# A four-layer transformer stack on one core: reciprocals spread by ScalarE, a shorter guess, a shorter matrix series

## The chip, the cores and the metric

One Trainium2 core. A core has five engines that run side by side, each with its own queue in order: TensorE (PE in the profile, with its weight loads as PEld), VectorE (DVE), ScalarE (ACT), GpSimd (POOL) and SyncE (SP, which issues DMAs). They meet only at semaphores. The metric is the device time of one execution in microseconds, lower is better.

## The reference

`x` is (32, 128, 144): 32 sequences of 128 tokens with 144 channels, all fp32. Four layers are applied one after the other, each conditioned on one vector per sequence:

```python
# layer 0: adaLN block; q and k are normalised per head (16 heads of 9)
qkv = (ln(x) * (1 + sc) + sh) @ w_qkv + b_qkv
q, k = ln(q) * g_q, ln(k) * g_k                 # over the 9 channels of a head
attn = softmax(q @ k.T * 9**-0.5)
x = x + g_msa * ((attn @ v) @ w_proj + b_proj)
x = x + g_mlp * (gelu(mod(ln(x)) @ w1 + b1) @ w2 + b2)

# layer 1: a rotation per sequence in a subspace of 64 directions
U, _ = qr(P)                                    # P is 144 x 64
R = expm(A)                                     # A: 64 x 64, skew, from the condition
x = x + (x @ U @ R - x @ U) @ U.T

# layers 2 and 3: adaLN blocks like layer 0 without the norm of q and k;
# layer 3 has a mixture of 4 experts, 2 per token, in place of the MLP
```

## The kernel before

The program is written in one recorded order, which every engine follows for its own instructions; no scheduler reorders it. The order comes from a table of *ticks*. In each tick three sequences are at three stages of attention: `s0` gets its first scores (for the row maxima), `s1` its second scores (maxima subtracted) and exponentials, `s2` its weighted sums and the projection out. One sequence enters each tick. Layer 0, here called the first block, takes 32 ticks and the few around them; layers 2 and 3 follow. A tick has named gaps ("a", "e", "b", "den", "c", "y1", "d", "z" and so on), and the table puts other work into them: layer norms, projections to q, k, v for later sequences, the MLP of earlier ones.

In a tick of the first block, after the second half of the scores (L841, with two reductions on VectorE, L846, and two exponentials on ScalarE, L853), gap "c" issues `qk0_T` for the next sequence (four transpositions, L771, and three scalings on ScalarE, L774 to L776) and `qk0_project` for a later one (L686 and L687 on TensorE, then two operations on ScalarE, L729 and L730). `divide_T` follows gap "c", `divide` follows gap "y1", `largest_T` and `largest` stand near the end, and `project_out` (L932) closes the tick.

The softmax division works in transposed form. `sums` transposes the weighted sums (L881), takes the reciprocals of the 16 denominators per token on VectorE (`rd`, L884) and spreads each one over the 16 columns of its slot (`rdx`, L886). `divide_T` transposes the spread tile back on TensorE (L906), into the bank of the sums, and `divide` multiplies (`oT`, L911). `project_out` uses `oT`.

The norm of q and k in layer 0 needs a reciprocal root per head. `qk0_variance` sums the squares, `qk0_guess` makes the integer guess (a shift right by one, then a subtraction from a constant, both on VectorE) and `qk0_newton` improves it three times on GpSimd.

Layer 1's matrices are prepared during the first block, in pieces. `prep_qr` makes the QR by 64 Householder columns, three pieces per column, six pieces per tick. `prep_expm` makes the matrix exponential: a scaling by a power of two (`THETA`, `NSQ`, `NSQ1`), the powers of the squared matrix, two series of eight terms (`even`, `odd`) in two halves of four (`hi`, `lo`), and four squarings (L561). It gets one piece in gap "b" and one in gap "z" of a tick; each `yield` ends a piece. A branch (L586) would add fourteen squarings if a matrix had a norm over `THETA * 2**4`. When both are done, `prep_rot` (L601) joins them; what is left by tick 30 is done there at once.

Of the kernel before, what the change touches and what calls it, by code (L numbers as in the profile page):

```python
# [8 lines left out]
F32 = mybir.dt.float32  # L9
U32 = mybir.dt.uint32  # L10
I32 = mybir.dt.int32
AF = mybir.ActivationFunctionType
ALU = mybir.AluOpType
# [20 lines left out]
EPS = 1e-6  # L34
SCALE = HD**-0.5

THETA = 2.0
NSQ = 18
NSQ1 = 4
KP = 80  # L40
# [10 lines left out]
SLOT = 16  # L51
ONE = HD
RSQRT = 0x5F3759DF
# [13 lines left out]
def tile_kernel(ctx: ExitStack, tc: tile.TileContext, a: dict, out: bass.AP):  # L67
    nc = tc.nc
# [4 lines left out]
    work = ctx.enter_context(tc.tile_pool(name="work", bufs=2))  # L73
# [45 lines left out]
    def mat(name, tag=None):  # L119

        tag = tag or name

        if tag in ("pow1", "pow2"):
            at0 = MLP_COLS + 1024 * (tag == "pow2")
            return mlps[:, at0 : at0 + 1024].rearrange("p (b d) -> p b d", d=D)
        if tag in ("pow3", "pow4"):
            return pw34[:, int(tag == "pow4")]
        if tag in ("hi", "even_lo"):
            at0 = 4 + 2 * (tag == "hi")
            t = hid[:, at0 : at0 + 2].rearrange("p a i t -> p (a i t)")  # L130
            return t.rearrange("p (b d) -> p b d", d=D)
        return pe.tile([128, NB2, D], F32, tag=tag, name=name)
# [261 lines left out]
    def prep_expm():  # L394
# [9 lines left out]
        i2b = cst[:, K_I2 : K_I2 + D].unsqueeze(1).to_broadcast([128, NB2, D])  # L404
# [102 lines left out]
        def products(lhs, rhs, name, take):  # L507

            for c in range(2):
                ps = bank([128, 512], f"{name}_{c}")  # L510
                product(ps, lhs, rhs, c)
                take(
                    slice(c * NB4, (c + 1) * NB4), ps.rearrange("p (b d) -> p b d", d=D)
                )
                yield

        fact = [1.0]
# [3 lines left out]
        pw1, pw2, pw3, pw4 = (mat(f"pow{n}") for n in range(1, 5))  # L521
# [5 lines left out]
        def series(co, name):  # L527

            lo, hi = mat(f"{name}_lo"), mat(f"{name}_hi", "hi")
            for t, cs_ in ((hi, co[4:]), (lo, co[:4])):  # L530
                nc.vector.tensor_scalar(t, pw1, cs_[1], None, ALU.mult)
                yield
                for c, x in ((cs_[0], i2b), (cs_[2], pw2), (cs_[3], pw3)):
                    nc.vector.scalar_tensor_tensor(t, x, c, t, ALU.mult, ALU.add)
                    yield
            yield from products(
                pw4, hi, f"ps_{name}",
                lambda bs, ps: nc.vector.tensor_tensor(lo[:, bs, :], lo[:, bs, :], ps, ALU.add),
            )
            return lo  # L540

        even = yield from series([(-1.0) ** k / fact[2 * k] for k in range(8)], "even")
        odd = yield from series([(-1.0) ** k / fact[2 * k + 1] for k in range(8)], "odd")
        rot, rotT = mat("rot", "pow3"), mat("rotT", "pow4")

        def sum_and_difference(bs, ps):
# [62 lines left out]
    st = defaultdict(dict)  # L609
# [129 lines left out]
    def qk0_guess(s):  # L739
        va = st[s]["va"]  # L740
        y = small.tile([128, 32], F32, tag="qky", name=f"qky_{s}", bufs=2)
        nc.vector.tensor_scalar(
            y.bitcast(I32), va.bitcast(I32), 1, None, ALU.logical_shift_right
        )
        nc.vector.tensor_scalar(y.bitcast(I32), y.bitcast(I32), -1, RSQRT, ALU.mult, ALU.add)
        st[s]["y"] = y

    def qk0_newton(s, eng=nc.gpsimd):
# [128 lines left out]
    def sums(s):  # L877

        po = st[s]["ot"][:, : 2 * T].rearrange("p (t q) -> p t q", t=2)
        for t in range(2):  # L880
            nc.tensor.transpose(po[:, t, :], st[s]["on"][:, t, :], ident)  # L881
        den = po.rearrange("p t (s c) -> p t s c", c=SLOT)[:, :, :, ONE]
        rd = small.tile([128, 2, 8], F32, tag="rd", name=f"rd_{s}")
        nc.vector.reciprocal(rd, den)  # L884
        rdx = work.tile([128, 2, 8, SLOT], F32, tag="rdx", name=f"rdx_{s}")
        nc.vector.tensor_copy(rdx, rd.unsqueeze(3).to_broadcast([128, 2, 8, SLOT]))  # L886
        st[s]["rdx"] = rdx

    def sums_by_blocks(s):

# [10 lines left out]

    def divide_T(s):
        po = st[s]["ot"][:, : 2 * T].rearrange("p (t q) -> p t q", t=2)
        rdx = st[s].pop("rdx")
        for t in range(2):
            nc.tensor.transpose(po[:, t, :], rdx[:, t, :, :].rearrange("p s c -> p (s c)"), ident)  # L906

# [215 lines left out]
    def load_L3():  # L1123

        t, at0 = rotU.rearrange("p b c -> p (b c)"), 0
        for k in ("wqk", "wqkR", "wv", "wvR", "wproj", "b2"):
# [11 lines left out]
            setattr(L3, k, v)  # L1138

    prep_qr, prep_expm = prep_qr(), prep_expm()  # L1140
    g2 = const.tile([128, 1], F32, name="g2")

# [40 lines left out]
    def prepare_expm(tick, gap):  # L1183
        nonlocal prep_expm
        if prep_expm and (tick >= 0 and gap in ("b", "z") or (tick, gap) == (-2, "z")):
            said = next(prep_expm, 0)
            if said == 0:
                prep_expm = None
            elif said is not None:
                rot_T.append(said)  # L1190
# [26 lines left out]
    for layer in range(3):  # L1217
        ahead = 5 if layer == 0 else 6
        for n in range(NG):
            g = (layer, n)  # L1220
            t0 = first[layer] + n * G
            for i in range(G):
                s = layer * B + n * G + i
# [17 lines left out]
                if layer == 0:  # L1241
                    put(t0 + i - 3, "c", qk0_project, s)
                    put(t0 + i - 3, "z", qk0_variance, s)
                    put(t0 + i - 2, "e", qk0_guess, s)
                    if s == 0:
                        for gap in "bbc":
                            put(-2, gap, qk0_newton, s, nc.vector)
                    else:
                        for gap in ("b", "c", "y2"):
                            put(t0 + i - 2, gap, qk0_newton, s)  # L1250
                    put(t0 + i - 1, "b", qk0_divide, s)
                    put(t0 + i - 1, "c", qk0_T, s)
# [62 lines left out]
    for tick in range(-6, first[2] + B + 14):  # L1315
# [20 lines left out]
        if s2 is not None and not joined:  # L1336
            sums(s2)
# [5 lines left out]
        if s2 is not None and not joined:  # L1343
            divide_T(s2)
# [30 lines left out]
def constants():  # L1375
# [9 lines left out]
    for h in range(2):  # L1385
        c[:, K_THR + h * NSQ + t] = np.where(t < NSQ1, -1.0, THETA * 2.0**t)
        c[:, K_WTS + h * NSQ + t] = -(2.0 ** -(t + 1.0))
# [136 lines left out]
```

## Time and profile before

| | |
|---|---|
| runs | 1351.33, 1355.53, 1358.17 us (median 1355.53) |
| profiled execution | 1347.1 us, span of the instructions 1345.4 us |
| TensorE | 1275.4 us busy (95%), weight loads 935.1 (70%) |
| VectorE | 821.9 us (61%) |
| ScalarE | 821.3 us (61%) |
| GpSimd | 642.6 us (48%) |
| granted TensorE clock, mean | 0.993 |

The three runs lie within 7 us of each other, and the profiled execution a little below them. Engines' busy times are over the whole span; the first block, with the preparation of layer 1 beside it, reaches to about 440 us of it. Matmuls are pipelined and the ends of their rows are modelled, so a busy TensorE is not one at its peak. In a line of the trace, `L906` is a line of the kernel, the tile written stands ahead of the arrow, and brackets tell how long the engine sat idle before it and what ended that.

### The profile page before, as it was taken

Reading aid. Unit: us, or ns where it says so; the run is one execution under the profiler, and the core shown is the slowest. Engines: PE = TensorE matmul, PEld = TensorE weight load, DVE = VectorE, ACT = ScalarE, POOL = GpSimd, SP = SyncE. Lnnn points to the kernel's source line nnn. Section 1 sums busy time; section 2 is a strip of 40 time slices with the busy share of each in tenths; the row PEclk is TensorE's granted clock in tenths of the full one; section 3 lists DMA queues with packets and bytes.
Section 4 is the critical chain, followed back from the end, with each engine's and each line's share of the span. In section 5 each row is a group of like instructions: output and inputs, shape, how many; then the busy total and the mean of one; then the engine's idle time right before and its main releaser. Section 6 shows DMA issues by size and latency. Waiting matters only on the chain.

```text
span 1345.4 us, 35550 instructions
## 1 busy us (share of the span) xinstructions
PE 1275.4 (95%) x14172; PEld 935.1 (70%) x14172; DVE 821.9 (61%) x2546; ACT 821.3 (61%) x1804; POOL 642.6 (48%) x1651
## 2 busy tenths in 40 slices
PE   5999898999999989999999999999999999999997
PEld 4678587787776566766777767667676767677765
DVE  5788888867754466666766676645454545454322
ACT  2667777778856565667766666655555555555431
POOL 5677777666644333433434343526261616151632
PEclk9999999999999999999999999999999999999999
DMA  8200000000020000000100000201000000000000
GB/s 235 51 2 19 20 19 2 20 20 4 19 100 31 19 11 19 19 10 19 53 15 15 19 19 9 76 1 28 1 24 5 19 10 19 10 19 2 19 9 9
DMA packets 21671, 34.40 MB, mean 26 GB/s; under 512 B 2304, under 2 KB 12448, under 8 KB 21248
## 3 DMA queue, kind: packets, MB, share of 16 engines
q1 hardware_dynamic: 20848, 31.68, 7.9%
q8 instruction: 114, 1.87, 0.6%
q10 hardware_dynamic: 656, 0.42, 0.1%
q14 instruction: 53, 0.43, 0.1%
HBM read 29.62 MB, written 2.47 MB: 24 GB/s over the span
## 4 chain that ended last, share of the span: by engine, by line
PE 66%; DVE 7%; ACT 1%; issue 1%; POOL 0%; POOLq 0%; DVEq 0%
PE ps_h L665 19%; PE ps_f L1085 8%; PE ps_s L841 6%; PE ps_qk L665 6%; PE ps_o L868 5%; PE ps_w L841 5%; PE ps_f L958 4%; DVE nm L846 3%; PE ps_pj L932 3%; PE ps_v L665 2%; PE ps_f L1089 1%; PE ps_o L800 1%; DVE block L897 1%; DVE oT L899 1%; DVE kT L719 1%
## 5 line engine op out<-in xcount | busy, mean ns | idle before, releaser
L846 DVE TENSOR_REDUCE nm<-ps_s 128x4 f32<-128x512 f32 x384 | 246.3, 682 | 88.4 <-PE ps_w L841 77.2
L853 ACT ACTIVATE pr<-ps_w 128x512 f32<-128x512 f32 x384 | 208.6, 595 | 134.4 <-PE ps_w L841 132.9
L841 PE MATMUL ps_w<-q,kT 32*128 32x128 f32 x3072 | 234.3, 284 | 0.9 <-DVE kT L719 0.9
L841 PE MATMUL ps_s<-kT,qT 32*128 32x256 f32 x1536 | 231.5, 406 | 0.7 <-ACT kT L776 0.6
L841 PEld LDWEIGHTS ps_w<-q,kT 32*128 32x128 f32 x3072 | 197.6, 187 | 12.8 <-issue 6.2
L952 ACT ACTIVATE hid<-ps_h 128x512 f32<-128x512 f32 (+1 forms) x224 | 119.1, 591 | 105.4 <-PE ps_h L665 105.2
L918 POOL TENSOR_TENSOR x_sb<-x_sb,res_a 128x144 f32<-128x144 f32 x96 | 47.1, 490 | 255.9 <-DVE res_a L921 255.1
L841 PEld LDWEIGHTS ps_s<-kT,qT 32*128 32x128 f32 x1536 | 135.1, 184 | 28.6 <-issue 8.2
L665 PE MATMUL ps_h<-hM_m,mlps 128*128 128x512 f32 x304 | 143.8, 606 | 0.0
L1093 DVE SCALAR_TENSOR_TENSOR acc<-ps_f,cw,acc 128x144 f32<-128x144 f32 x128 | 46.6, 366 | 158.6 <-PE ps_f L1089 72.2
L868 PE MATMUL ps_o<-pr,vaug 128*32 128x128 f32 x3072 | 104.8, 277 | 0.6 <-issue 0.6
L868 PEld LDWEIGHTS ps_o<-pr,vaug 128*32 128x32 f32 x3072 | 78.6, 110 | 34.9 <-PE ps_w L841 18.5
L665 PEld LDWEIGHTS ps_h<-hM_m,mlps 128*128 128x128 f32 x304 | 53.5, 190 | 65.6 <-issue 64.2
L958 PE MATMUL ps_f<-mlps,hid 128*128 128x144 f32 x640 | 93.3, 293 | 0.0
L958 PEld LDWEIGHTS ps_f<-mlps,hid 128*128 128x128 f32 x640 | 82.5, 191 | 7.5 <-issue 4.0
L655 ACT ACTIVATE hM_m<-ps_hT_m,modM 128x128 f32<-128x128 f32 x96 | 44.5, 464 | 63.5 <-PE ps_hT_m L653 63.3
L626 POOL TENSOR_SCALAR rs_m_a<-mv_m_a 128x2 f32<-128x2 f32 x81 | 15.7, 193 | 137.2 <-DVE mv_m_a L624 109.7
L918 POOL TENSOR_TENSOR x_sb<-x_sb,res_m 128x144 f32<-128x144 f32 x64 | 32.6, 510 | 97.0 <-DVE res_m L921 96.9
L853 ACT ACT_TABLE_LOAD x57 | 73.1, 1283 | 7.0 <-PE ps_w L841 6.2
L949 ACT ACT_TABLE_LOAD x58 | 74.4, 1283 | 1.0
L1085 PEld LDWEIGHTS ps_f<-pair,hid 128*128 128x128 f32 x512 | 67.2, 191 | 8.4 <-issue 7.7
L1085 PEld LDWEIGHTS ps_f<-mlps,hid 128*128 128x128 f32 x512 | 67.2, 191 | 8.0 <-issue 6.9
(318 smaller groups left out, 2926.6 us busy)
## 6 DMA issues: line engine op xcount, KB each, us to landing
gates<-gates SPq DMA_DIRECT2D x48, 288.0 KB, 3.5
x_sb<-in_x SPq DMA_DIRECT2D x8, 288.0 KB, 9.1
out_x<-x_sb SPq DMA_DIRECT2D x8, 288.0 KB, 2.6
mlps<-in_L_mlp SPq DMA_DIRECT2D x2, 1000.0 KB, 6.2
pair<-in_L_mlp SPq DMA_DIRECT2D x1, 1800.0 KB, 10.7
mlps<-in_L_mlp SPq DMA_DIRECT2D x1, 1800.0 KB, 8.2
pow<-in_W SPq DMA_DIRECT2D x4, 320.0 KB, 6.6
mlps<-in_L_wmod SPq DMA_DIRECT2D x4, 290.0 KB, 4.8
```

The lines of the kernel that those rows point to most:

```text
L655: nc.scalar.activation(gr[g][f"{k}_{kind}"][:, i, :], ps[:, k == "hR", :], AF.Identity, bias=m[:, sh, b : b + 1], scale=m[:, sc, b : b + 1],)
L665: nc.tensor.matmul(ps, x, y, start=k == 0, stop=k == 1)
L841: nc.tensor.matmul(o, x, y, start=True, stop=True)
L846: nc.vector.tensor_reduce(nmv[:, at0 : at0 + 2, ONE : ONE + 2], view.rearrange("p (r t k) -> p r t k", t=2, k=T), AX.X, ALU.max, negate=True,)
L853: nc.scalar.activation(pr[:, 4 * e : 4 * e + 4, :].rearrange("p s q -> p (s q)"), view, AF.Exp, scale=SCALE,)
L868: nc.tensor.matmul(po[rows4(j), t, :], v[:, 4 * j + 2 * t + r, :], prs[j // 2][:, 4 * (j % 2) + 2 * r + t, :], start=r == 0, stop=r == 1,)
L918: nc.gpsimd.tensor_tensor(x_sb[:, b, :], x_sb[:, b, :], t, ALU.add)
L949: nc.scalar.activation(t, half, AF.Gelu_apprx_tanh)
L952: nc.scalar.activation(hid[:n, i], ps[:n], AF.Gelu_apprx_tanh)
L958: nc.tensor.matmul(ps, hid[:, at0, i, :], w2[:, m, :], start=m == 0, stop=m == NFC - 1)
L1085: nc.tensor.matmul(ps[:, 0, :], hid[:, at0 + m, i, :], w2[:, at0 + m, :], start=m == 0, stop=m == 3)
L1093: nc.vector.scalar_tensor_tensor(acc, ps[:, 0, :], w, acc, ALU.mult, ALU.add)
```

## The change

It has three parts. The spread of the reciprocals leaves `sums` on VectorE and is issued in `divide_T` on ScalarE. The guess is one multiplication by -0.5 and an addition, in place of a shift and a multiplication by -1 with the addition. The two series have seven terms in place of eight, the first operation of each half (a multiplication of `pw1`) is issued on ScalarE, and `THETA` is 1.75 in place of 2. Each series is one piece shorter.

```diff
-THETA = 2.0
+THETA = 1.75
...
             for t, cs_ in ((hi, co[4:]), (lo, co[:4])):
-                nc.vector.tensor_scalar(t, pw1, cs_[1], None, ALU.mult)
+                nc.scalar.mul(t, pw1, cs_[1])
                 yield
-                for c, x in ((cs_[0], i2b), (cs_[2], pw2), (cs_[3], pw3)):
+                for c, x in zip(cs_[:1] + cs_[2:], (i2b, pw2, pw3)):
                     nc.vector.scalar_tensor_tensor(t, x, c, t, ALU.mult, ALU.add)
                     yield
...
-        even = yield from series([(-1.0) ** k / fact[2 * k] for k in range(8)], "even")
-        odd = yield from series([(-1.0) ** k / fact[2 * k + 1] for k in range(8)], "odd")
+        even = yield from series([(-1.0) ** k / fact[2 * k] for k in range(7)], "even")
+        odd = yield from series([(-1.0) ** k / fact[2 * k + 1] for k in range(7)], "odd")
...
     def qk0_guess(s):
-        nc.vector.tensor_scalar(
-            y.bitcast(I32), va.bitcast(I32), 1, None, ALU.logical_shift_right
-        )
-        nc.vector.tensor_scalar(y.bitcast(I32), y.bitcast(I32), -1, RSQRT, ALU.mult, ALU.add)
+        nc.vector.tensor_scalar(y.bitcast(I32), va.bitcast(I32), -0.5, RSQRT, ALU.mult, ALU.add)
...
     def sums(s):
         nc.vector.reciprocal(rd, den)
-        rdx = work.tile([128, 2, 8, SLOT], F32, tag="rdx", name=f"rdx_{s}")
-        nc.vector.tensor_copy(rdx, rd.unsqueeze(3).to_broadcast([128, 2, 8, SLOT]))
-        st[s]["rdx"] = rdx
+        st[s]["rd"] = rd
...
     def divide_T(s):
         po = st[s]["ot"][:, : 2 * T].rearrange("p (t q) -> p t q", t=2)
-        rdx = st[s].pop("rdx")
+        rdx = work.tile([128, 2, 8, SLOT], F32, tag="rdx", name=f"rdx_{s}")
+        nc.scalar.copy(rdx, st[s].pop("rd").unsqueeze(3).to_broadcast([128, 2, 8, SLOT]))
         for t in range(2):
             nc.tensor.transpose(po[:, t, :], rdx[:, t, :, :].rearrange("p s c -> p (s c)"), ident)
```

## The prediction, made before the result was known

> **What bounds the kernel now.** I read the page first, then the busy times by stretch, then the waits, then single ticks in order of time. The change touches the first block alone, which ends near 440 us. Its stretches (us; busy time of TensorE, its weight loads, VectorE, ScalarE, GpSimd; granted clock; DMA):
>
> ```profile
> 60.00:130.00 70.00, 65.10 (x1008) 53.44 (x997) 62.40 (x219) 50.40 (x147) 51.42 (x155) 0.98 0.03 11
> 130.00:250.00 120.00, 110.82 (x1319) 85.39 (x1319) 103.08 (x327) 84.84 (x229) 88.53 (x229) 0.97 0.05 17
> 250.00:320.00 70.00, 68.69 (x1220) 53.73 (x1220) 50.14 (x178) 57.35 (x146) 42.18 (x129) 1.00 0.03 11
> 320.00:440.00 120.00, 113.30 (x1276) 85.39 (x1277) 73.46 (x253) 81.60 (x198) 63.87 (x186) 1.00 0.14 46
> ```
>
> TensorE is full in all four; VectorE is close behind it up to 250 us (165 of 190) and has a third free after that. So TensorE paces the block, and VectorE does where TensorE waits for it. How often that is, the waits tell (us in total, times, longest):
>
> ```profile
> PE ps_qr L327 <- DVE at L353: 7.8, 6, 2.4
> PE ps_pj L932 <- DVE oT L911: 7.4, 8, 1.1
> ```
>
> These two are nearly all of it: TensorE and its weight loads together leave 22 us uncovered between the first and the last of the 32 starts of L906, and in 14 of those 31 ticks nothing at all. L906, the transposition of the spread reciprocals, is the place to look at. One full tick (start, length):
>
> ```profile
> 97.71 1.09 ACT L853 ACTIVATE pr<-ps_w 128x512 f32<-128x512 f32 x2 [0.76 <-PE ps_w L841]
> ...
> 98.52 0.65 PE L687 MATMUL ps_qk<-L_wqkR,hR_a 128*128 128x288 f32 x2
> 98.69 0.48 ACT L774 ACTIVATE qT<-ps_qkT,g 128x256 f32<-128x256 f32 x1
> ...
> 98.76 0.39 PEld L906 LDWEIGHTS ps_o<-cst,rdx 128*128 128x128 f32 x2
> ...
> 99.40 0.49 ACT L776 ACTIVATE kT<-ps_qkT,cst 128x256 f32<-128x256 f32 x1
> 99.42 1.01 PEld L501 LDWEIGHTS ps_mlps<-mlps 64*64 64x64 f32 x32 [0.17 <-PE ps_o L906]
> ...
> 99.76 0.43 ACT L729 COPY qkraw<-ps_qk 128x288 f32<-128x288 f32 x1
> ...
> 100.01 0.41 DVE L911 TENSOR_TENSOR oT<-on,ps_o 128x256 f32<-128x256 f32 x1
> 100.03 0.46 ACT L730 ACTIVATE qksq<-ps_qk 128x288 f32<-128x288 f32 x1
> ```
>
> TensorE begins L906 at 98.76, straight behind the projection L687. ScalarE is then at the third of seven operations, and ends the last of them, qksq, at 100.49: 1.73 us later.
>
> **The change, part by part.** Durations (ns: least, median, most, then mean for the last row):
>
> ```profile
> L886 DVE COPY rdx<-rd x32: 293/295/393, 63.9 to 430.3; 128x256 f32<-128x256 f32 x32
> L742 DVE TENSOR_SCALAR qky<-qkv x32: 147/149/183, 24.1 to 380.9; 128x32 int32<-128x32 int32 x32
> L531 DVE TENSOR_SCALAR hid<-mlps x3: 679/683/683, 130.8 to 191.8; 128x1024 f32<-128x1024 f32 x3
> L534 DVE SCALAR_TENSOR_TENSOR hid<-pow,hid x3: 1268/1269/1506, 147.7 to 210.3; 128x1024 f32<-128x1024 f32 x3
> ```
> ```profile
> L874 ACT COPY on<-ps_o 128x256 f32<-128x256 f32 x32 | 12.0, 376 | 7.5 <-PE ps_o L868 7.5
> ```
>
> *The spread, moved.* Off VectorE: 32 x 0.295 us. On ScalarE it is issued in divide_T, after everything that gap "c" issued. So ScalarE's order in a full tick is two exponentials, three scalings of qT and kT, qkraw, qksq, and only then the spread: it stands behind the exponentials and behind five more. TensorE's order does not change: L906 comes right after the projection and now waits for all seven. Behind L906 in TensorE's queue stand largest_T, the MLP's matrices, the products of the exponential series, project_out, the next column of the QR and the next tick's scores. VectorE waits with oT (L911), which needs L906.
>
> Its price: in each tick, the end of ScalarE's last operation ahead of the spread less the start of L906, read from the trace. Twenty-two ticks give 1.15 to 1.74 us (mostly 1.7), five with a late table load ahead of the exponentials 2.3 to 2.9, one 3.3, two with exponentials alone 1.3, one 0.2, the last nothing: 55.5 us. The spread itself has no row on ScalarE. The nearest is L874, the same 128x256, from PSUM, 0.376 us, of which 0.1 overlaps its predecessor as neighbours there do (qkraw at 99.76 for 0.43, qksq at 100.03): 0.27 us, times 31 = 8.4. Its bounds: 0.2 (one of 128x144, L794, is 0.30 less the overlap) and 0.5 (one of 128x512 is 0.60 less it): 6 to 15 us. Stall of TensorE: 55.5 + 8.4 = 64 us.
>
> What hides it: only time in which TensorE already waits between this L906 and the next. Taken tick by tick (the lesser of stall and idle), that is 20.5 us of the 22; the rest of the cover doesn't exist, because a full TensorE shifts whole and the shifted exponentials start as much later in the next tick. Net +43. If nothing were absorbed, since oT is late too: +64. If matmuls had hidden slack and half vanished: +20.
>
> *What VectorE gains.* The guess loses L742: 0.149 us, about 0.19 from start to start, 32 times. The series lose four first terms (4 x 0.68) and two products (2 x 1.27): 5.3 us. With the spread, 9.4 + 6.1 + 5.3 = 21 us. TensorE's waits for VectorE can repay it, but the stall has already taken them, save 1.4 us in the few ticks where they are longer than the stall (1.0 of it in the tick from 64.86). I take -1; bounds 0 and -21, the latter if VectorE paced every tick.
>
> *Four first terms on ScalarE, 128x1024.* No row; two of 128x512 take 1.19 us, which bounds one from above. Two stand in gap "b" ahead of the QR's L338, two behind the spread. L338 had 30.6 us of idle time before it over 53 issues, which covers them. Nothing; uncovered, 4.8 us.
>
> *Two yields fewer.* The exponential's pieces run one tick earlier from the series on. The last one, L592, ran at 326.4, and its reader, L601, at 379.8, held by the QR: no gain. Moved squarings meet other MLP steps: 0, give or take 2.
>
> *THETA.* Thresholds become 1.75 x 2^t. The largest row sum of the skew matrices, worked out from the reference's inputs, is 26.77; it stays below 28 as below 32, so the branch with fourteen more squarings stays untaken. Nothing.
>
> *Clock.* From 130 to 250, where TensorE idled most, the granted clock was 0.97, else 1.00. With a stall in each tick the 190 us after 250 may fall to 0.97 too: 0 to +6; I take +2.
>
> Sum: +43 - 1 + 2 = +44. The profiled execution took 1347.1 us (span 1345.4), so 1391; the median of the three runs shown is 8.4 us higher than it, so 1399 for a median.
>
> Two rules of the Trainium skill, weighed. The row: weight loads are busy 278 of the 380 us from 60 to 440, matmuls 358. "Perfetto Trace Analysis", section "Identifying the Most-Contended Engine", calls matmul busy time a bad measure and weight-load time the good one; by it 102 us would be free, enough to swallow the whole stall, and the sum would be near +0. I go by the tick above, where queued TensorE work follows without a mark of idle time. The row: the clock dipped in the early stretches, in which TensorE's longest waits were 1 to 3 us. "TensorE: Matmul & The Clock Gate", "Why this matters for your kernels", has the clock fall after gaps over about 3 us; stalls of 2 us would then add nothing, which makes the sum +42.
>
> **Rivals.**
> 1. *Slower, less: slack.* TensorE's lengths are modelled, and half of the shift vanishes: +15 to +25, 1371 to 1381. For it: the weight loads' share. Against: 14 ticks without a gap.
> 2. *Faster: VectorE decides.* If ticks end with VectorE's queue, the 21 us come back at 0.5 us or more a tick. Place: ticks up to 250, where VectorE idled as little as 0.7 us in 10 to 12. It decides once waits of TensorE behind L906 exceed the stall of 2 us in most ticks; they do in three or four. Price: -5 to -21, 1335 to 1351.
> 3. *No change:* gain and stall cancel, 1349 to 1362; needs a stall of 0.6 us a tick, that is, a spread that overtakes the five operations. ScalarE's order forbids that.
> 4. *The branch is taken:* fourteen squarings, 64 products each (32 take 1.15 us) and four copies of about 0.7: 14 x 5 = 70 us, 1425. Needs a row sum over 28.
>
> **How the numbers follow.** Stall at full price 0.80 (1380 to 1420), slack 0.11, faster 0.05, no change 0.03, branch 0.01. The range takes in most of the slack case and the unabsorbed stall: 1371 to 1420. No change means within 0.5% (7 us), about what can be told here. Faster 0.06, same 0.03, slower 0.91.
>
> **What would show it.** Right: in full ticks L906 follows the spread at once, TensorE has an idle mark of 1.4 to 2.1 us there, put down to ScalarE; the block ends near 480 instead of 440; after it, nothing differs. VectorE's busy time falls by some 20 us, ScalarE's rises by 12 + 4. Wrong: the idle mark at L906 is under 1 us, or waits at L932 and L327 shrink by more than 22 us, or the clock halves for long. I would be wrong if the scores' matmuls, not ScalarE's seven operations, set when L906 can run.

## The result and the profile after

The changed kernel takes 1412.95 us (median of 4 runs, 1410.08 to 1418.51) against 1355.49 before: 1.0429 times the time, 95% interval 1.0387 to 1.0471, so 57.5 us slower. The forecast was slower, to 1399, within 1371 to 1420. For one kernel below, the spread twice, the ratio leaves out the slowest of four executions, which is also the profiled one.

Its profiled execution took 1418.5 us, its span 1416.8. It is the slowest of the four, and the profiled execution before (1347.1) was 8 us faster than the median, so the profiles lie 71 us apart where the medians lie 57.5. The same stretches of the first block, which now ends near 510 us (columns as before):

```profile
60.00:130.00 70.00, 60.27 (x886) 46.26 (x884) 54.71 (x190) 46.50 (x139) 46.01 (x139) 0.98 0.06 16
130.00:250.00 120.00, 100.78 (x1195) 77.17 (x1195) 84.59 (x269) 82.83 (x221) 77.03 (x202) 0.93 0.04 12
...
390.00:510.00 120.00, 100.03 (x1031) 71.22 (x1031) 52.35 (x177) 71.40 (x167) 48.97 (x143) 0.96 0.14 47
510.00:930.00 420.00, 404.21 (x4711) 288.13 (x4707) 268.06 (x747) 270.80 (x534) 164.64 (x404) 0.98 0.07 22
```

TensorE, which was covered for 93% of the first stretch, is covered for 86%. No engine took over as the bound: VectorE fell from 62 to 55 us of 70, ScalarE from 50 to 47. All of them wait more, and the waits of the block say for what (in us in total, times, longest):

```profile
PEld ps_o L902 <- ACT rdx L900: 76.0, 32, 4.3
PE ps_o L902 <- ACT rdx L900: 62.1, 32, 3.8
...
DVE oT L907 <- PE ps_o L902: 52.0, 30, 7.8
```

L902 is the former L906, the transposition of the spread reciprocals, and L900 is the spread, now on ScalarE. The wait did not exist before; it comes 32 times out of 32 and holds up oT on VectorE in turn. One full tick, the fourth with a transposition, which is the one that the prediction shows (start, length):

```profile
105.47 0.65 PE L687 MATMUL ps_qk<-L_wqkR,hR_a 128*128 128x288 f32 x2
105.64 0.48 ACT L771 ACTIVATE qT<-ps_qkT,g 128x256 f32<-128x256 f32 x1
...
106.70 0.43 ACT L729 COPY qkraw<-ps_qk 128x288 f32<-128x288 f32 x1
106.98 0.46 ACT L730 ACTIVATE qksq<-ps_qk 128x288 f32<-128x288 f32 x1
107.28 0.45 ACT L900 COPY rdx<-rd 128x256 f32<-128x256 f32 x1
107.79 0.44 PE L902 MATMUL ps_o<-cst,rdx 128*128 128x128 f32 x2 [1.67 <-ACT rdx L900]
...
108.26 0.42 DVE L907 TENSOR_TENSOR oT<-on,ps_o 128x256 f32<-128x256 f32 x1 [1.24 <-PE ps_o L902]
```

Where TensorE went from the projection straight to the transposition, it now stands 1.67 us behind the projection's last row, and ScalarE works through qT, kT, qkraw and qksq without a pause until it gets to the spread.

Between the profiles, 71.4 us of span split in three: 7.8 up to the first transposition of rdx (start-up loads; this start lies anywhere from 65 to 82 us in the profiles of this study), 59.0 between the first and the last of the 32 (370.1 before, 429.1 after), and 4.6 behind it. The middle part is nearly the whole loss. I call it the block's length below, since it is free of the start's scatter.

### The profile page after: what moved, and what is told of

Read it like the earlier page. It is cut to its first block, busy times and chain, and to the rows that moved or that the text cites. A ratio compares the mean times of both kernels' runs of the same rounds, so it can differ in the third digit from the quotient of the medians.

```text
span 1416.8 us, 35464 instructions
## 1 busy us (share of the span) xinstructions
PE 1297.7 (92%) x14172; PEld 946.3 (67%) x14172; DVE 804.8 (57%) x2476; ACT 833.5 (59%) x1840; POOL 639.9 (45%) x1651
## 4 chain that ended last, share of the span: by engine, by line
PE 65%; DVE 6%; ACT 3%; issue 1%; POOL 0%; POOLq 0%
PE ps_h L665 18%; PE ps_f L1081 8%; PE ps_s L838 6%; PE ps_qk L665 5%; PE ps_o L865 5%; PE ps_w L838 5%; PE ps_f L954 4%; PE ps_pj L928 3%; DVE nm L843 2%; PE ps_v L665 2%; PE ps_f L1085 1%; PE ps_o L797 1%; DVE block L892 1%; DVE oT L894 1%; ACT pr L850 1%
## 5 line engine op out<-in xcount | busy, mean ns | idle before, releaser
L838 PE MATMUL ps_s<-kT,qT 32*128 32x256 f32 x1536 | 236.3, 414 | 0.1
L838 PEld LDWEIGHTS ps_s<-kT,qT 32*128 32x128 f32 x1536 | 139.2, 190 | 29.1 <-issue 8.4
```

The costliest lines, as they stand in the source:

```text
L838: nc.tensor.matmul(o, x, y, start=True, stop=True)
```

## Experiments

Theory: TensorE's order keeps the transposition right behind the projection, ScalarE's order puts the spread behind seven operations, and TensorE, which paces the block, stands still for the difference. Rivals: the other two parts cost; ScalarE is too slow or too full for the spread wherever it stands; the halved clock that came with the gaps.

**The spread alone.** The kernel before, with this part only:

```diff
-        rdx = work.tile(...); nc.vector.tensor_copy(rdx, rd...)     # in sums
+        rdx = work.tile(...); nc.scalar.copy(rdx, rd...)            # in divide_T
```

> The kernel before with one part of the change: the spread of the reciprocals on ScalarE, issued in divide_T. Theory (the spread stands behind seven operations of ScalarE, and TensorE stalls at it in each tick): nearly the whole loss, 1403 to 1420 us for a median against 1355 before, and TensorE idle 55 to 70 us ahead of the transpositions of rdx. Rival (the shorter series, moved to ScalarE and shifted by a tick, or the guess, cost a good part): under 1395 us.

1411.7 us, 1.0458 (1.0402 to 1.0515); block 424.0; TensorE waits 59.8 us at the transpositions. The whole loss is in this part.

**All but the spread.** The changed kernel with `rdx` spread on VectorE in `sums` again.

> The changed kernel with the spread back on VectorE: the guess in one instruction, seven terms, first terms on ScalarE and THETA stay. Theory: the 11 us that VectorE saves repay only where TensorE waits for VectorE (22 us of idle time in the first block), so -1 to -6 us against before: 1349 to 1355. Rival (these parts cost): over 1362 us.

1353.0 us, 1.0003 (0.9970 to 1.0037). The expected few microseconds of gain are not to be told from nothing. The block is 1.9 us shorter in the profile. One thing in it was not expected: the tick with the branch of the matrix exponential. Before, from the waits:

```profile
PE ps_pj L932 <- DVEq L586: 1.1, 1, 1.1
```

And in this run:

```profile
PE ps_pj L929 <- PEq L586: 3.9, 1, 3.9
```

With the series two pieces shorter, the branch falls into another tick, and TensorE stands 2.8 us longer at it. In the spread-alone run, where the pieces are as before, it is 1.1 us; in every run with the short series 3.7 to 4.2. So this part takes 2.8 us there and, the block being 1.9 us shorter all the same, gives some 4 to 5 elsewhere; the medians show neither.

**The spread on ScalarE, straight behind the exponentials.**

```diff
         scores(s0, s1, 1)
+        if s2 is not None and not joined:
+            spread(s2)                  # nc.scalar.copy(rdx, rd...)
         fill(tick, "c")
```

> The changed kernel with the spread on ScalarE issued ahead of gap c, straight behind the two exponentials and ahead of the five operations of qk0_T and qk0_project. Theory (place in ScalarE's queue decides): in a full tick of the trace before, the second exponential ends 0.04 us after TensorE reaches the transposition, and the spread took 0.45, so the stall shrinks from some 2.1 to 0.4 us a tick: 1350 to 1368 us, at the middle 1360. Rival (ScalarE is too slow or too full for this operation, wherever it stands): over 1385 us. Rival (the clock, which was halved for 3 to 10 us at a time twelve times in the profile after, is the larger part): the halved stretches go with the stall, or stay and the time stays over 1375.

1364.2 us, 1.0099 (1.0065 to 1.0133); block 379.9. The same instruction on the same engine, five places further ahead in its queue, gives back 44 of 57 us. What it still waits for:

```profile
L899 ACT COPY rdx<-rd x32: 399/405/453, 71.2 to 447.0; 128x256 f32<-128x256 f32 x32
...
  PE ps_o L906: 12.7, 11
```

The time is as expected, the way to it is not: in place of 0.4 us in each tick, 21 transpositions wait for nothing and 11 wait 0.3 to 2.3 us. ScalarE's load is the same as in the changed kernel, so load is not the price.

**The spread on ScalarE, ahead of the exponentials** (`spread(s2)` right behind `sums(s2)`).

> The changed kernel with the spread on ScalarE issued in sums, ahead of the tick's second pair of exponentials. Theory: VectorE's reciprocal is done 1.2 us ahead of the exponentials in ticks that TensorE paces, so the spread hides there, and TensorE doesn't wait for it; in ticks that VectorE paces the reciprocal comes up to 0.9 us behind the time the exponentials could start, and the exponentials then wait for it. Sum: 1343 to 1360 us, at the middle 1352. Rival (the exponentials, held up in each tick, hold up everything): over 1370 us.

1354.6 us, 1.0008 (0.9978 to 1.0038); block 368.5; TensorE waits 0.6 us at the transpositions in all, while ScalarE itself stands 12.7 us for the reciprocal, at no cost. So the spread can be on ScalarE for nothing; and nothing is also what it brings.

**The same place, the other engine.** The spread in `divide_T`, on VectorE:

```diff
-        nc.scalar.copy(rdx, st[s].pop("rd")...)
+        nc.vector.tensor_copy(rdx, st[s].pop("rd")...)
```

> The changed kernel with the spread issued in divide_T, but on VectorE: the same place in the program, another queue. There it stands behind the tick's two reductions (L846 before), of which the second ends 0.12 us behind TensorE's arrival in full ticks and about 1 us in ten others. Theory (what stands ahead of the spread in its queue is the price): 1360 to 1375 us. Rival (the engine is the price): within 3 us of the kernel before.

1361.2 us, 1.0045 (1.0013 to 1.0078); block 373.3. With two reductions ahead of it rather than seven operations, the wait is 6.5 us in all. The loss itself is small: the interval is 1.8 to 10.6 us, so by time alone the rival's 3 us are not excluded; the wait, which was 0.4 us with the spread in `sums` on the same engine, is what tells the place from the engine. The order is that of the ends of what stands ahead: sums, VectorE's reductions, ScalarE's exponentials, ScalarE's gap c.

**Useless work in the gap.** Ahead of the transpositions of `rdx`, into an unused part of the bank:

```diff
+        for n in range(14):
+            nc.tensor.transpose(st[s]["ot"][:, (2 + n % 2) * T : (3 + n % 2) * T], ident, ident)
```

> The changed kernel with fourteen transpositions of the identity into an unused part of the bank, ahead of the transpositions of rdx: 1.5 us of TensorE work that nobody reads, laid into the 1.7 us gap of each tick. Theory (TensorE waits there for ScalarE and for nothing else): the idle time ahead of the transposition falls from 62 to some 10 to 20 us, and the time stays within 10 us of the changed kernel's. Rival (the halved clock, which the gaps bring on, makes up the 15 us by which the loss was larger than predicted): the halved stretches fall from 58 us to under 25, and the time falls by 8 to 17 us.

1413.7 us, 1.0422 (1.0367 to 1.0476): fourteen transpositions more in each of 32 ticks, and the time of the changed kernel. The wait falls from 62.1 to 13.3 us. TensorE's room is in this gap, and it cannot be used by what stands behind. The rival's drop of 8 to 17 us did not come, but neither did its condition: from 60 us on, the halved stretches in the profile fell from 58 us to 31, not under 25, and the mean clock of the four executions is 0.981 to 0.986, where the changed kernel has 0.977 to 0.982. So the time of this run does not settle the clock's part. The two profiles, laid side by side from transposition to transposition, say more: 23 of the 31 ticks are equally long within 0.02 us, and the block is 6.3 us shorter mainly by five ticks in which the clock was halved for less time or not at all (7.8 us; the tick of the branch is 1.4 us longer). The medians do not show these 6 us.

**The spread twice.**

```diff
-        nc.scalar.copy(rdx, rd...)
+        for _ in range(2):
+            nc.scalar.copy(rdx, rd...)
```

> The changed kernel with the spread written twice in a row on ScalarE. Theory: ScalarE's end of the chain sets TensorE's next start in each tick, so each tick grows by the second spread's 0.35 to 0.45 us: 11 to 14 us more than the changed kernel, 1422 to 1430 us. Rival (TensorE's wait is set by something else and the spread only happens to lie there): within 4 us of the changed kernel.

1.0658 (1.0580 to 1.0736), some 89 us over the kernel before and 31 over the changed one, where 11 to 14 were expected. In its profile, of the execution at 1458.7 us, the granted clock from 130 to 250 us is 0.84. Against the profile of the changed kernel, the six ticks with no halved clock in either are 0.44 us longer each, which is the second spread; thirteen ticks with one more halved stretch of 3.4 us are 1.65 to 2.14 us longer, so such a stretch costs up to half its length. The block is 36.0 us longer: 31 times 0.44 is 13.6, and 22 are the clock. The clock is what the theory did not cover, so the gap was filled here too.

**The spread twice, gap filled** (the same, with eighteen transpositions of the identity ahead of those of `rdx`).

> The kernel with the spread written twice, which came out 37 us over the changed one and not 11 to 14, with 116 us of halved clock in its profile against 58; here eighteen transpositions of the identity fill the gap ahead of the transposition of rdx. Theory (the longer gaps bring the halved clock on, and that is the excess): halved stretches under 60 us, and 1422 to 1435 us. Rival (the excess comes from ScalarE's own chain, whatever the clock does): over 1440 us.

1423.6 us, 1.0490 (1.0440 to 1.0540): less time with more work. The stretch from 130 to 250 us of the run with the spread twice, and below it that of this run:

```profile
130.00:250.00 120.00, 100.66 (x1136) 77.39 (x1134) 75.58 (x244) 75.48 (x202) 70.33 (x186) 0.84 0.03 11
```
```profile
130.00:250.00 120.00, 111.27 (x1405) 90.36 (x1404) 83.84 (x273) 86.24 (x232) 78.24 (x208) 1.00 0.04 12
```

The mean clock was 0.964 to 0.974 in the three executions behind the ratio, and 0.984 to 0.993 here. So of the 31 us, 8 (by the ratios) to 11 (by the medians) are the second spread on the path, where 11 to 14 were expected, and 20 to 23 are the clock. The two profiles agree: the block is 465.1 us with the spread twice and 434.5 here, and ticks with no halved clock in either are equally long within 0.06 us, though each holds eighteen transpositions more here.

**The transpositions later, first try.** `divide_T` and `divide` behind gap "d" and `largest_T` (the conditions are left out):

```diff
-        divide_T(s2)
         fill(tick, "y1")
-        divide(s2)
         fill(tick, "y2")
         fill(tick, "d")
         largest_T(s0, ...)
+        divide_T(s2)
+        divide(s2)
```

> The changed kernel with divide_T and divide issued behind gap d and largest_T, so that TensorE has the MLP's pieces of gap d to do while ScalarE gets to the spread. Theory: in three ticks of four the MLP work of 1.2 to 2.4 us hides the wait, but project_out then waits 0.8 us for oT; in the fourth nothing is there to hide it. Between 1370 and 1395 us. Rival (the load of ScalarE, not TensorE's wait in order, costs the time): over 1403 us.

1413.7 us, 1.0442 (1.0385 to 1.0499), a miss, and the fault of the edit: the spread is issued in `divide_T` and moved along, behind the gelu's table load in one tick of four. It told neither theory from the other.

**Only the transpositions later** (the spread stays behind gap "c").

> The changed kernel with the spread left in its place in ScalarE's queue (behind gap c), and only TensorE's transpositions of rdx, with the multiplication to oT, moved behind gap d and largest_T. (In the run with both moved, the spread came to stand behind the gelu's table load in one tick of four, so it told two things at once.) Theory (TensorE loses what it has nothing else to do in): ticks with MLP pieces in gap d hide the wait, the eight early ticks and one later tick in four do not, and project_out waits 0.3 us for oT: 1368 to 1392 us. Rival (it is ScalarE's load): over 1403 us.

1400.9 us, 1.0328 (1.0279 to 1.0377); block 409.1. Better than the changed kernel, and between the two expectations: above the theory's range and 2 us under the rival's, so the time alone does not part them. The wait for `rdx` halves, from 62.1 to 30.2 us, but project_out, which is now close behind, waits 9.9 us for oT where it waited 2.3; the clock, at 0.971 to 0.979, is no better either. The waits show that half of the gap stayed and a part of the rest moved; ScalarE's load is that of the changed kernel, and the block is 20 us shorter, so the load does not set the time. How much of what is left is the clock I did not separate.

**VectorE's time spent on TensorE's work.** The runs say that TensorE paces and that VectorE's savings are worth nothing by themselves. So I spent them: the kernel with the short guess and series and the spread on VectorE, where from tick 18 the division goes by VectorE's own transpositions, as in the later layers.

```diff
-        if s2 is not None and not joined:
+        blocks = tick >= 18
+        if s2 is not None and not blocks:
             sums(s2)
         fill(tick, "pre1")
-        if s2 is not None and joined:
+        if s2 is not None and blocks:
             sums_by_blocks(s2)
...
```

> A version that follows from the theory: TensorE paces, VectorE has time to spare once the series are done. The kernel with the guess and the series changed and the spread on VectorE, where from tick 18 of the first block on the division goes by sums_by_blocks (VectorE's own transpositions, as the later layers do), so that TensorE drops the four transpositions of L881 and L906, 0.11 us each. Theory: 17 ticks x 0.44 = 7 us less, 1343 to 1351 against 1353 to 1356 before. Rival (VectorE's longer chain delays the maxima or oT and eats it): 1352 to 1362 us.

1351.0 us, 0.9953 (0.9921 to 0.9985): 6.4 us less than before, 7 expected. The stretch from 250 to 440 us, before and then with this edit:

```profile
250.00:440.00 190.00, 181.99 (x2496) 139.12 (x2497) 123.60 (x431) 138.95 (x344) 106.05 (x314) 1.00 0.10 33
```
```profile
250.00:440.00 190.00, 178.89 (x2467) 135.92 (x2469) 132.84 (x444) 142.46 (x355) 112.50 (x325) 0.98 0.10 34
```

VectorE does 9 us more in it and has 57 to spare. The two stretches are not quite the same work, since the block starts 10 us later here. From the end of the 16th `project_out` to the end of the 32nd it is 195.7 us before and 190.2 here, with VectorE busy for 127 and 133 of it. It beats both kernels, by little: 0.9953 of the time before, with 1 outside the interval, though the interval (up to 2 us under before) reaches into the rival's range.

**The same from tick 10.**

> The same from tick 10 on, eight ticks earlier, into the stretch in which VectorE was busy 103 of 120 us in the trace before. Theory: in these ticks the 0.85 us more of VectorE's time come onto the path in half of them, so no better than from tick 18: 1346 to 1357 us. Rival (VectorE has room there too, since the series are shorter): another 3.5 us less than from tick 18.

1353.4 us, 0.9972 (0.9944 to 1.0000): no better than from tick 18, as expected where VectorE is nearly full, though the two intervals overlap.

The block's length, in the profiles that can be compared, and all idle time of TensorE ahead of the transpositions of rdx (us):

| kernel | block | wait for rdx | time against before |
|---|---|---|---|
| before | 370.1 | 0.0 | 1 |
| all but the spread | 368.2 | 0.4 | 1.0003 |
| ScalarE, ahead of the exponentials | 368.5 | 0.6 | 1.0008 |
| VectorE, in divide_T | 373.3 | 6.5 | 1.0045 |
| ScalarE, behind the exponentials | 379.9 | 12.7 | 1.0099 |
| only the transpositions later | 409.1 | 30.2 | 1.0328 |
| gap filled | 422.8 | 13.3 | 1.0422 |
| the spread alone | 424.0 | 59.8 | 1.0458 |
| the change | 429.1 | 62.1 | 1.0429 |

## Why the prediction was right, and by how much it was off

*The mechanism* was right: the spread stands behind five operations more than the exponentials; TensorE's order does not give way; it waits in each tick; and behind the block only 4.6 us are lost. The block before and after, the spread alone and the three other places for the spread show it. The signs came as forecast, or near: an idle mark of 1.67 us in full ticks (1.4 to 2.1), VectorE's busy time 17 us less (20), ScalarE's 12 more (16).

*The price of a full tick* was nearly right. A tick counted from one transposition to the next ends with the wait of the second. Paired so, the 14 ticks in which TensorE had no idle time before were forecast to grow by 31.3 us together and grew by 28.7, seven of them by 1.78 to 1.89 each where 2.0 stood in the forecast. The forecast counted the stall from the start of the weight load, which came 0.24 us ahead of its matmul (98.76 and 99.00 in the tick shown). The spread itself, put at 0.376 us by the copy of the same shape from PSUM, took 0.45; with its overlap, and the 0.05 until TensorE began, that is 0.34 against 0.27, inside the bounds given.

*Two ticks were misread.* The stall was put at 0.2 us for the transposition at 390.50 and at nothing for the last, at 434.97. In the trace before, ScalarE's last operations ahead of the spread's place end 1.64 and 2.33 us behind these starts:

```profile
391.63 0.51 ACT L776 ACTIVATE kT<-ps_qkT,cst 128x256 f32<-128x256 f32 x1
...
436.02 1.28 ACT L713 ACTIVATE kT<-ps_qk,cst 128x512 f32<-128x512 f32 x2
```

TensorE waited 1.71 and 2.60 us there, almost 4 us more than was put down.

*The mis-sized term* is what hides the stall: "that is 20.5 us of the 22". 8.4 of the 22 are left in the block after, so 13.4 vanished. What is left stands mainly at the branch (3.7) and at `project_out`, which still waits 0.4 us for oT in six ticks (2.3), since oT is late too. The branch was put at "0, give or take 2": it moved from the tick at 315 us into that at 305, which grew by 5.6 where 1.9 was forecast.

*The clock* was put at +2 and took more. (It was also misread: outside 130 to 250 us it was not 1.00 throughout, as the row from 60 to 130 has 0.98.) In the block after, 44 us are at halved clock against 10 before. The time in which TensorE is covered grew by 12 us: by 3 in the 20 ticks that have no halved clock in either profile, and by 9 in the other eleven. Filling the gap took 6.3 us off the block, all in ticks with halved clock. So some 6 to 9 us of the block are the clock, in these profiles; in the medians it does not show. Behind the block the halved stretches reach to 599 us after, and the tail is 4.6 us longer.

Together: 60.4 us of new idle time ahead of the 31 transpositions that end a tick of the block, less the 13.4 that vanished, and 12 of covered time make the 59.0 measured; the forecast for stall and hiding was 64 - 20.5 = 43.5. The range held because it reached up to the stall with nothing hidden. The estimate in it was 14 us low, as what hides, the two ticks and the clock all erred to the same side.

*VectorE's gain* was put at -1 with 21 as the other bound, and is nothing that can be measured (1.0003 and 1.0008). *The first terms on ScalarE* took 1.09 us each and cost nothing to be seen. *THETA* did nothing: TensorE has 14172 matmuls in both profiles, so the fourteen squarings stayed out.

*The rivals.* Slack in TensorE is out: its idle time is in the gap, where useless work fits for nothing, and not behind it. The Trainium skill ("Perfetto Trace Analysis", "Identifying the Most-Contended Engine") judges TensorE's headroom by weight-load time, beside the share of peak arithmetic. By weight loads 102 us were free, and the change would have cost nothing; the block grew by 59. Here the order of the queue decides and not the free time. VectorE as the pace is out by the run with all but the spread.

## What to carry to other kernels

Work moved to an engine with idle time is priced by what stands ahead of it in that engine's queue at the point of issue, compared with the moment its reader gets there; "behind the exponentials" was five operations too late, and the same copy ahead of them was free. Time taken off an engine that does not pace is worth nothing until it is spent on work of the one that does.

## What was not expected of the hardware

TensorE's clock was halved after gaps well under 3 us, and the more often the longer the gap was. A halved stretch in these traces lasts 3.4 us, or two or three times that. I counted after which of the 32 waits ahead of the transpositions one began, within 4.5 us of the wait's end:

| idle time ahead of the transposition | kernel | followed by halved clock |
|---|---|---|
| under 0.5 us | gap filled; spread twice, gap filled | 0 of 48 |
| 0.7 to 2.3 us | the same two | 5 of 16 |
| 1.4 to 1.7 us | the change | 2 of 24 |
| 2.2 to 2.9 us | the change | 4 of 6 |
| over 3 us | the change | 2 of 2 |
| 1.8 to 2.2 us | the spread twice | 16 of 24 |
| 2.6 to 2.7 us | the spread twice | 2 of 3 |
| over 3 us | the spread twice | 5 of 5 |

The gaps need not come in every tick: the kernel before has a halved stretch at 524.5 us, behind a single gap of 2.1 us. In all, the profile before has 17 us of halved clock (its last microseconds left out), the changed kernel's 58, that of the spread twice 116, in its slowest execution. Filling the gaps there with transpositions that nobody reads brought this to 17 us in the profile, the mean clock of the executions from 0.964 to 0.974 up to 0.984 to 0.993, and the time close to the expected one. The Trainium skill ("TensorE: Matmul & The Clock Gate", "Why this matters for your kernels") warns of gaps over about 3 us; the runs show a price below that. At 1.7 us in a full tick, filling took 6.3 us off the block in the profile and nothing that the medians show.
